# Four graph layers on one core: moving the small steps of each layer norm from GpSimd to VectorE and ScalarE

## The chip, the core and the metric

The kernel runs on one core of a Trainium2 chip. A core has TensorE for matmuls (PE in the profile; its weight loads are the row PEld), VectorE (DVE), ScalarE (ACT), GpSimd (POOL) and SyncE (SP), which here issues most of the DMA transfers. The metric is the time of one execution on the device, in microseconds (us). The kernel before the change takes 5522.48 us, the median of three runs (5521.77 to 5525.03). Everything is float32.

## The reference

A batch of 128 graphs, each with 128 nodes of 512 features, goes through four layers. Each layer adds its result to its input and then normalises every row. Cut to what matters here:

```python
def _layernorm(x, axis=-1, eps=1e-5):
    m = jnp.mean(x, axis=axis, keepdims=True)
    v = jnp.var(x, axis=axis, keepdims=True)
    return (x - m) / jnp.sqrt(v + eps)

def hypergraph_conv(x, adj, W, b):            # used twice in layer 1
    H = (adj != 0).astype(x.dtype)
    w = adj.reshape(N, -1)[:, :C]             # the first row of adj
    xw = jnp.einsum('ncd,hd->nch', x, W)
    Dn = jnp.einsum('nce,ne->nc', H, w);  Dn = jnp.where(Dn > 0, 1.0 / Dn, 0.0)
    Be = H.sum(axis=1);                   Be = jnp.where(Be > 0, 1.0 / Be, 0.0)
    m = Be[:, :, None] * jnp.einsum('nce,nch->neh', H, xw)
    return Dn[:, :, None] * jnp.einsum('nce,neh->nch', H, m) + b

# layer 1
h = jax.nn.relu(hypergraph_conv(x, adj, W1, b1))      # 1024 wide
h = layer_norm(h, gamma, beta)                        # a norm inside the layer
y = hypergraph_conv(h, adj, W2, b2)
x = _layernorm(x + (y + x))
# layers 0, 2 and 3 (two attention-like graph layers and one of 8 heads): x = _layernorm(x + layer(x, adj))
```

Each graph therefore has five norms (one for each layer and one inside layer 1), 640 in all, each over 128 rows, one row in a partition.

## The kernel before

The program works on pairs of graphs (`U = 2`), 64 pairs, and two pairs at a time. Matrix products are done by Strassen's scheme, which trades matmuls for additions: GpSimd builds sums of the left operands (`operands`, `lefts`), and VectorE or ScalarE takes each product out of PSUM into its block of the result.

The instructions are not issued in the order of the source. A `Plan` records every operation with its engine, an estimate of its length and its dependencies; a list scheduler then plays all engines forward and puts each engine's instructions in a fixed order. Every operation is emitted from one line (L369), so the profile is read by the names of tiles, not by lines. A name such as `four`, `first`, `out`, `ks` or `rows` is a piece of memory that holds different things at different times; `col` holds numbers, one or a few to each row; `bank` and `t` are PSUM.

The norm, and the part of it that GpSimd has:

```python
def norm_terms(st, n=1):
    mv = col(2)
    ve.bn_aggr(mv, st[:, :6 * n])                                   # mean, variance
    rstd = col(1)
    po.tensor_scalar(rstd, mv[:, 1:2], EPS, None, op0=OP.add)
    po.tensor_tensor(rstd, rstd, neghalf, OP.pow)                   # (var + eps) ** -0.5
    nmr = col(1)
    po.tensor_scalar(nmr, mv[:, 0:1], rstd, -1.0, op0=OP.mult, op1=OP.mult)
    return nmr, rstd

def layer_norm(t):
    st = col(12)
    stats(st, 0, t)                                                 # ve.bn_stats
    nmr, rstd = norm_terms(st)
    ac.activation(t, t, AF.Identity, bias=nmr, scale=rstd)          # rstd * t - mean * rstd
```

Layer 1 (`...` marks cuts). `drds` holds, for each row, the factor of `bw2`, which is the row that `beta` gives behind `W2`:

```python
def prepare1():
    ...
    sp.dma_start(b2h, rows(b2, D))
    ve.tensor_scalar(b2h, b2h, 0.5, None, op0=OP.mult)
    ...
def layer1(i0):
    ...
        for b in range(U):          # HT = (adj != 0), cnt = its sums
            ve.tensor_scalar(HT[:, b], AT[:, b], 0.0, None, op0=OP.not_equal, op1=OP.add,
                                    accum_out=cnt[:, b:b + 1])
        po.tensor_scalar(cnt, cnt, 1.0, None, op0=OP.max)
        po.tensor_tensor(cnt, cnt, minus1, OP.pow)
        HB = sq(M)
        for b in range(U):
            po.tensor_scalar(HB[:, b, :P], HT[:, b], cnt[:, b:b + 1], None, op0=OP.mult)
    ...
        for b in range(U):          # the inner part of the layer, on h of 1024
            t = h[r][b].rearrange("p g f -> p (g f)")
            ve.scalar_tensor_tensor(t, t, dns[r][b], rows1[:, :2]..., op0=OP.mult, op1=OP.add)
            ac.activation(t, t, AF.Relu)
            ...                     # bn_stats of two halves
            nmr, rstd = norm_terms(sts, 2)
            ac.activation(t, t, AF.Identity, bias=nmr, scale=rstd)
    ...
        q = four()
        for b in range(U):
            po.tensor_tensor(x1[:, b], x1[:, b], b2h, OP.add)
            ac.mul(q[:, b], bw2, drds[r][:, b:b + 1])
            ve.scalar_tensor_tensor(q[:, b], x1[:, b], 2.0, q[:, b], op0=OP.mult, op1=OP.add)
        for b in range(U):
            p = bank()
            pe.matmul(p, K[:, b, :P], G[:, b], start=True, stop=True)
            ve.scalar_tensor_tensor(q[:, b], p, dns[r][b], q[:, b], op0=OP.mult, op1=OP.add)
            layer_norm(q[:, b])
```

Of the kernel before, what the change touches and what calls it, by code (L numbers as in the profile page):

```python
# [14 lines left out]
OP = mybir.AluOpType  # L15
# [3 lines left out]
D = 512  # L19
# [6 lines left out]
EPS = 1e-5  # L26
U = 2
# [9 lines left out]
WHENT = (.8, 2.1), (2.0, 3.1)  # L37
WHEN1 = (-3.0, -2.3, -1.6, -1.1, .2, .6)
STEP1 = .22
WHENH, WHENW, WHENG = (2.4, 3.0), (2.8, 3.5), (3.4, 4.1)  # L40
WHEN2 = (-2.4, -2.0, -1.45, -1.15, -.7, .3, .5, 2)
WHENV, WHENS, WHENP, WHENO = (.9, 1.9), (2.2, 3.2), (3, 4), (3.5, 4.5)
LAG1, LAG2 = 1, 1.5
# [74 lines left out]
def estimate(engine, name, out, args, kw):  # L118

    n = out.idx.size if isinstance(out, View) else 0  # L120
    views = [a for a in args if isinstance(a, View)]
    psum = any(a.tile.kind in PSUM for a in views)
    scalars = sum(isinstance(a, View) and a.idx.size == 1 for k, a in [*enumerate(args), *kw.items()] if k != "accum_out")
    if engine == PE:
        return 107 if name == "transpose" else (1.74 if n <= P else 1.68) * n
    if name == "dma_start":
        return ISSUE
    if engine == DVE:
        if name == "bn_aggr":
            return 75  # L130
        if name == "reciprocal":
            return 67 + 6.5 * n
        if name in ("tensor_reduce", "bn_stats"):
            n = views[0].idx.size
        fast = name in ("tensor_scalar", "tensor_copy") and not psum and "accum_out" not in kw
        return 67 + n / (1.92 if fast else .96) + (61 * scalars if n > 8 else 0)
    if engine == ACT:
        return 50 + n / 1.2 + (0 if psum else 43) + 92 * scalars + 94 * ("accum_out" in kw)
    if name == "tensor_tensor":
        return 500 + 35 * n if OP.pow in args else 150 + 2.1 * n if n < 800 else 1.82 * n  # L140
    return 40 if name == "memset" else 180 + 3.2 * n if n > 8 else 180


def shares_port(engine, name, args, kw):
# [227 lines left out]
def rows(ap, n):  # L372

    return bass.AP(tensor=ap.tensor, offset=ap.offset, ap=[[0, P], [1, n]])
# [3 lines left out]
def kernel(  # L378
# [41 lines left out]
    for kind, k, t in (*(("out", k, t) for k, t in enumerate(outs)), ("w28", 0, places["w28"][0]),  # L420
                       ("row1", 0, places["row1"][0])):
        for c in range(SIZE[kind] // SIZE["four"]):
# [3 lines left out]
    pe, ve, ac, po, sp = (plan.engine(*e) for e in ((PE, nc.tensor), (DVE, nc.vector), (ACT, nc.scalar),  # L426
                                                     (POOL, nc.gpsimd), (SP, nc.sync)))

    def tile_of(kind, *shape):
        n = math.prod(shape)  # L430
        flat = View(Tile(kind), np.arange(SIZE[kind]))[:, :n]
        names = [f"a{k}" for k in range(len(shape))]
        return flat if len(shape) == 1 else flat.rearrange(
            f"p ({' '.join(names)}) -> p {' '.join(names)}", **dict(zip(names, shape)))

    def fixed(*shape, name, kind="fixed"):
        t = const.tile([P, *shape], FP, name=name)
        return View(Tile(kind, t), np.arange(math.prod(shape)).reshape(shape))
# [4 lines left out]
    def four():  # L443

        return tile_of("four", U, D)
# [4 lines left out]
    def col(*n):  # L450
        return tile_of("col", *n)
# [3 lines left out]
    ident = View(Tile("fixed", ident_), np.arange(P))  # L455
    neghalf = fixed(1, name="neghalf")
    po.memset(neghalf, -0.5)
    minus1 = fixed(U, name="minus1")
    po.memset(minus1, -1.0)
    tiny = fixed(1, name="tiny")  # L460
    po.memset(tiny, 1e-12)
    junk = fixed(D, name="junk", kind="free")
# [1 line left out]
    def dot(dst, u, v, n=D):  # L464
        ve.scalar_tensor_tensor(junk[:, :n], u, 1.0, v, op0=OP.mult, op1=OP.mult, accum_out=dst)
# [25 lines left out]
    def seven(nk, nh):  # L491

        return tile_of("w28", 7, nk, nh)

    def combine(W, on=ve):

        on.tensor_tensor(W[:, T3], W[:, B22], W[:, B12], OP.subtract)
        on.tensor_tensor(W[:, T1], W[:, B12], W[:, B11], OP.subtract)
        on.tensor_tensor(W[:, T2], W[:, B22], W[:, T1], OP.subtract)
        on.tensor_tensor(W[:, N4], W[:, B21], W[:, T2], OP.subtract)  # L500
# [140 lines left out]
    def norm_terms(st, n=1):  # L641
        mv = col(2)
        ve.bn_aggr(mv, st[:, :6 * n])
        rstd = col(1)
        po.tensor_scalar(rstd, mv[:, 1:2], EPS, None, op0=OP.add)
        po.tensor_tensor(rstd, rstd, neghalf, OP.pow)
        nmr = col(1)
        po.tensor_scalar(nmr, mv[:, 0:1], rstd, -1.0, op0=OP.mult, op1=OP.mult)
        return nmr, rstd

    def layer_norm(t):
# [315 lines left out]

    rows1 = tile_of("row1", 4, D)
    b1_b = [rows1[:, k] for k in range(2)]
    b2h = rows1[:, 2]  # L970
    bw2 = rows1[:, 3]

    def prepare1():
        for g in range(2):
            sp.dma_start(b1_b[g], rows(b1[g * D:(g + 1) * D], D))
        sp.dma_start(b2h, rows(b2, D))
        ve.tensor_scalar(b2h, b2h, 0.5, None, op0=OP.mult)
        WT["w1"] = Seven([four() for _ in range(7)])
        yield from load_T(WT["w1"], [w1], 2, D)
        for k, j in enumerate((B11, B21, T2, T1, B22, T3, N4)):  # L980
            yield
            WT["w1"].tiles[j] = Split(WT["w1"].tiles[j], tile_of("q3", 3, 2 * P))
            combine(WT["w1"].tiles[j], (ve, po)[k % 2])
        WT["w1"] = WT["w1"].tiles
        gb = four().rearrange("p u f -> p (u f)")
        sp.dma_start(gb, rows(gamma, DH))
        bb = four().rearrange("p u f -> p (u f)")
        sp.dma_start(bb, rows(beta, DH))
        cols = fixed(C, name="cols1")
        two = fixed(C, 2, name="two")  # L990

        def gamma_beta(o, st):
            for g in range(2):
                dot(two[:, o, g:g + 1], st[:, g * D:(g + 1) * D], bb[:, g * D:(g + 1) * D])
            ve.tensor_tensor(st, st, gb, OP.mult)

        WT["w2"] = seven(4, D // 2)
        yield from load_T(WT["w2"], [w2], 4, D // 2, gamma_beta, True)
        ve.tensor_reduce(cols, two, AX.X, OP.add)
        spread(bw2, cols)  # L1000

    def each(*lists):

        base = plan.key
        for r, args in enumerate(zip(*lists)):
            plan.key = base + r
            yield args

    def layer1(i0):
# [5 lines left out]
        for (_, ab), in each(loaded):  # L1015
            AT = sq()
            turned(AT, ab)
            HT = sq()
            cnt = col(U)
            for b in range(U):  # L1020
                ve.tensor_scalar(HT[:, b], AT[:, b], 0.0, None, op0=OP.not_equal, op1=OP.add,
                                        accum_out=cnt[:, b:b + 1])
            po.tensor_scalar(cnt, cnt, 1.0, None, op0=OP.max)
            po.tensor_tensor(cnt, cnt, minus1, OP.pow)
            HB = sq(M)
            for b in range(U):
                po.tensor_scalar(HB[:, b, :P], HT[:, b], cnt[:, b:b + 1], None, op0=OP.mult)
            po.tensor_copy(HB[:, :, P:P + 1], AT[:, :, 0:1])
            po.memset(HB[:, :, P + 1:P + 2], 1.0)
            HTs.append(HT)  # L1030
            HBs.append(HB)
        yield
        Ks, kept, dns, drds = [], [], [], []
# [42 lines left out]
        for r, i in enumerate(both):  # L1076
            plan.key = base + STEP1 * (5, 7)[r]
            for b in range(U):
                t = h[r][b].rearrange("p g f -> p (g f)")
                ve.scalar_tensor_tensor(t, t, dns[r][b], rows1[:, :2].rearrange("p g f -> p (g f)"),  # L1080
                                        op0=OP.mult, op1=OP.add)
# [4 lines left out]
                nmr, rstd = norm_terms(sts, 2)  # L1086
                ac.activation(t, t, AF.Identity, bias=nmr, scale=rstd)
                loads.append(through_dram(h[r][b].rearrange("p (j g) (k w) -> p j (g k) w", j=1, k=2), f"h{i + b}"))
        for r, i in enumerate(both):
            plan.key = base + WHENH[r]  # L1090
            hT = []
            for b in range(U):
                t = four().rearrange("p g (c n) -> p g c n", n=P)
                turned(t.rearrange("p g c n -> p (g c) n"), loads[U * r + b]())
                hT.append(t)
            ops = operands(hT[0][:, 0], hT[0][:, 1], hT[1][:, 0], hT[1][:, 1])
            plan.key = base + WHENW[r]
            G = four()
            strassen(ops, WT["w2"], 4, D // 2, plain_take(*halves(G)))
            plan.key = base + WHENG[r]  # L1100
            x1 = load_rows(x1d[i // U])
            K = tile_of("k", U, M)
            sp.dma_start(K.rearrange("p b n -> p (b n)"), kept[r], run=U * M)

            q = four()
            for b in range(U):
                po.tensor_tensor(x1[:, b], x1[:, b], b2h, OP.add)
                ac.mul(q[:, b], bw2, drds[r][:, b:b + 1])
                ve.scalar_tensor_tensor(q[:, b], x1[:, b], 2.0, q[:, b], op0=OP.mult, op1=OP.add)
            for b in range(U):  # L1110
                p = bank()
# [3 lines that stand above are left out]
            sp.dma_start(x2d[i // U], q)  # L1115
# [213 lines left out]
    n = B // U  # L1329
# [57 lines left out]
```

## Time and profile before

The profiled execution has a span of 5528.7 us at a mean TensorE clock of 0.992.

| engine | busy, us | share of the span | instructions |
|---|---|---|---|
| PE, matmuls | 5368.3 | 97% | 29145 |
| PEld, weight loads | 4254.2 | 77% | 29145 |
| DVE | 4386.7 | 79% | 10018 |
| ACT | 2317.8 | 42% | 5967 |
| POOL | 4585.9 | 83% | 6372 |

The layers follow each other with some overlap. Layer 0 ends and layer 1 begins around 1330 us, layer 1 gives way to layers 2 and 3 around 3080 us, and those two run together to the end. Two things help in reading. A busy time counts a stretch once, also where two instructions overlap; the mean length of a group counts each instruction whole. And a float32 matmul stands in the trace as two records, so that a count of matmuls there is twice that of the program.

### The profile page before, as it was taken

What the parts mean: (1) busy time and instruction counts of PE and PEld (TensorE: products, weight loads), DVE (VectorE), ACT (ScalarE), POOL (GpSimd) and SP (SyncE); (2) the same over time, 40 slices, a digit from 0 to 9 for tenths busy, and PEclk for the clock granted to TensorE, in tenths of its full rate; (3) what the DMA queues carried; (4) which work ended last, traced back from release to release, by engine and by line L of the source; (5) the groups of instructions that cost most, each with busy time, mean ns of one, the idle gap of its engine ahead of it and who ended that gap; (6) DMA issues with size and microseconds to landing.
All of it is one profiled execution on the core that took longest, in us unless ns stands there. A gap on an engine that the chain in (4) does not pass through costs nothing.

```text
span 5528.7 us, 93993 instructions
## 1 busy us (share of the span) xinstructions
PE 5368.3 (97%) x29145; PEld 4254.2 (77%) x29145; DVE 4386.7 (79%) x10018; ACT 2317.8 (42%) x5967; POOL 4585.9 (83%) x6372
## 2 busy tenths in 40 slices
PE   8999999999899999999999899999999999999998
PEld 4555555555688888888888788888898889898897
DVE  6787888877888888888788877777777777877776
ACT  2333333333344444444444334444444444444444
POOL 6777777767899999999999778888888888888886
PEclk8999999999999999999999999999999999999999
DMA  3333333334454545454545545555555555555553
GB/s 91 105 96 97 100 97 104 98 106 120 127 161 132 167 134 162 130 167 134 162 132 160 167 132 161 153 160 154 156 165 153 155 163 151 159 164 153 155 152 124
DMA packets 788378, 768.33 MB, mean 139 GB/s; under 512 B 264859, under 2 KB 592547, under 8 KB 787878
## 3 DMA queue, kind: packets, MB, share of 16 engines
q1 hardware_dynamic: 786374, 759.71, 45.8%
q8 instruction: 232, 3.80, 0.3%
q10 hardware_dynamic: 1504, 2.62, 0.2%
q14 instruction: 268, 2.20, 0.1%
HBM read 435.83 MB, written 326.24 MB: 138 GB/s over the span
## 4 chain that ended last, share of the span: by engine, by line
PE 76%; POOL 7%; DVE 6%; DMA 5%; issue 3%; ACT 2%; SPq 1%; POOLq 0%; DVEq 0%; ACTq 0%
PE bank L369 58%; PE t L369 18%; POOL out L369 2%; POOL four L369 2%; DVE first L369 2%; DVE out L369 2%; POOL col L369 1%; DVE col L369 1%; POOL first L369 1%; DMA out<-h 1%; SPq L369 1%; DVE four L369 1%; DMA four<-in_x_dram 1%; DMA four<-h 1%; DVE sq L369 1%
## 5 line engine op out<-in xcount | busy, mean ns | idle before, releaser
L369 PE MATMUL bank<-first,four 128*128 128x386 f32 (+3 forms) x4804 | 1464.8, 449 | 40.9 <-DVE out L369 23.1
L369 PEld LDWEIGHTS bank<-first,four 128*128 128x128 f32 (+2 forms) x4804 | 852.8, 189 | 601.1 <-DVE out L369 138.0
L369 DVE TENSOR_TENSOR out<-bank,out 128x386 f32<-128x386 f32 (+1 forms) x1968 | 960.3, 505 | 333.8 <-PE bank L369 250.0
L369 DVE TENSOR_TENSOR first<-bank,first 128x256 f32<-128x256 f32 x1351 | 546.3, 415 | 141.7 <-PE bank L369 122.9
L369 POOL TENSOR_TENSOR out<-out 128x256 f32<-128x256 f32 (+3 forms) x355 | 417.3, 1186 | 234.5 <-DVE out L369 187.2
L369 PE MATMUL bank<-first,out 128*128 128x256 f32 (+3 forms) x2414 | 560.7, 372 | 15.0 <-DVE first L369 8.5
L369 PEld LDWEIGHTS bank<-first,out 128*128 128x128 f32 (+2 forms) x2414 | 418.4, 187 | 105.6 <-DVE first L369 16.7
L369 ACT COPY out<-bank 128x258 f32<-128x258 f32 (+2 forms) x520 | 213.8, 417 | 646.6 <-PE bank L369 550.1
L369 POOL TENSOR_TENSOR col<-col,neghalf 128x1 f32<-128x1 f32 x640 | 384.1, 605 | 10.6
L369 POOL TENSOR_TENSOR four<-four,four 128x256 f32<-128x256 f32 (+2 forms) x445 | 377.6, 851 | 7.7 <-PE bank L369 0.7
L369 PE MATMUL bank<-four,out 128*128 128x256 f32 (+2 forms) x1568 | 381.0, 367 | 1.2 <-DVE first L369 0.8
L369 DVE TENSOR_TENSOR four<-bank,four 128x256 f32<-128x256 f32 x645 | 263.7, 415 | 141.1 <-PE bank L369 132.0
L369 PE MATMUL bank<-out,first 128*128 128x128 f32 (+3 forms) x2148 | 357.0, 309 | 13.1 <-ACT ks L369 2.6
L369 POOL TENSOR_TENSOR first<-first 128x512 f32<-128x512 f32 (+3 forms) x264 | 302.4, 1161 | 77.1 <-DVE first L369 56.1
L369 PE MATMUL bank<-four,first 128*128 128x128 f32 (+3 forms) x2144 | 362.9, 310 | 2.7 <-DVE rows L369 0.9
L369 ACT ACTIVATE four<-four,col,col 128x512 f32<-128x512 f32 x262 | 211.0, 812 | 312.4 <-POOL col L369 279.0
L369 POOL TENSOR_SCALAR col<-col 128x1 f32<-128x1 f32 (+1 forms) x704 | 185.4, 268 | 180.6 <-DVE col L369 136.1
L369 PEld LDWEIGHTS bank<-out,first 128*128 128x128 f32 (+2 forms) x2148 | 289.2, 186 | 45.5 <-issue 6.7
L369 PEld LDWEIGHTS bank<-four,first 128*128 128x128 f32 (+2 forms) x2144 | 301.1, 189 | 27.8 <-DVE ks L369 1.5
L369 PE MATMUL bank<-four,four 128*128 128x256 f32 (+2 forms) x1156 | 291.8, 371 | 13.2 <-DVE first L369 11.9
L369 POOL TENSOR_TENSOR four<-four 128x256 f32<-128x256 f32 (+2 forms) x375 | 275.1, 746 | 35.3 <-DVE four L369 27.9
L369 PEld LDWEIGHTS bank<-four,out 128*128 128x128 f32 (+2 forms) x1568 | 263.9, 188 | 40.4 <-issue 3.2
(448 smaller groups left out, 13190.6 us busy)
## 6 DMA issues: line engine op xcount, KB each, us to landing
h<-first SPq DMA_DIRECT2D x496, 128.0 KB, 2.6
out<-x1d SPq DMA_DIRECT2D x94, 512.0 KB, 5.0
out<-h SPq DMA_DIRECT2D x79, 512.0 KB, 4.8
four<-in_x_dram SPq DMA_DIRECT2D x512, 64.0 KB, 2.0
four<-in_x_dram SPq DMA_DIRECT2D x63, 512.0 KB, 4.0
x1d<-four SPq DMA_DIRECT2D x63, 512.0 KB, 2.8
first<-S SPq DMA_DIRECT2D x55, 512.0 KB, 4.2
four<-h SPq DMA_DIRECT2D x49, 512.0 KB, 4.7
```

The costliest lines, as they stand in the source:

```text
L369: call(*map(real, args), **{n: real(a) for n, a in kw.items()})
```

## The change

Of the small steps of each norm only the power stays on GpSimd. The addition of eps and the change of the mean's sign go to VectorE, in place, and the product of the mean and the inverse deviation goes to ScalarE. In layer 1, the inverse of the counts is made by VectorE with a maximum and a reciprocal. The row that is added to each node there (`b2` and the multiple of `bw2`) is built by one VectorE instruction, which takes the place of an addition on GpSimd and a product on ScalarE. The aim is to free GpSimd of many short instructions. The estimates that the scheduler uses and two of its starting times in layer 1 are changed with it, so that the order of the instructions is dealt anew on every engine.

```diff
-WHENH, WHENW, WHENG = (2.4, 3.0), (2.8, 3.5), (3.4, 4.1)
+WHENH, WHENW, WHENG = (2.4, 3.0), (2.9, 3.6), (3.6, 4.3)
...
         if name == "bn_aggr":
-            return 75
+            return 95
...
-    return 40 if name == "memset" else 180 + 3.2 * n if n > 8 else 180
+    return 60 if name == "memset" else 180 + 3.2 * n if n > 8 else 215
...
     def norm_terms(st, n=1):
         mv = col(2)
         ve.bn_aggr(mv, st[:, :6 * n])
+        ve.tensor_scalar(mv[:, 1:2], mv[:, 1:2], EPS, None, op0=OP.add)
+        ve.tensor_scalar(mv[:, 0:1], mv[:, 0:1], -1.0, None, op0=OP.mult)
         rstd = col(1)
-        po.tensor_scalar(rstd, mv[:, 1:2], EPS, None, op0=OP.add)
-        po.tensor_tensor(rstd, rstd, neghalf, OP.pow)
+        po.tensor_tensor(rstd, mv[:, 1:2], neghalf, OP.pow)
         nmr = col(1)
-        po.tensor_scalar(nmr, mv[:, 0:1], rstd, -1.0, op0=OP.mult, op1=OP.mult)
+        ac.mul(nmr, mv[:, 0:1], rstd)
         return nmr, rstd
...
-            po.tensor_scalar(cnt, cnt, 1.0, None, op0=OP.max)
-            po.tensor_tensor(cnt, cnt, minus1, OP.pow)
+            ve.tensor_scalar(cnt, cnt, 1.0, None, op0=OP.max)
+            ve.reciprocal(cnt, cnt)
...
             for b in range(U):
-                po.tensor_tensor(x1[:, b], x1[:, b], b2h, OP.add)
-                ac.mul(q[:, b], bw2, drds[r][:, b:b + 1])
+                ve.scalar_tensor_tensor(q[:, b], bw2, drds[r][:, b:b + 1], b2_b, op0=OP.mult, op1=OP.add)
                 ve.scalar_tensor_tensor(q[:, b], x1[:, b], 2.0, q[:, b], op0=OP.mult, op1=OP.add)
```

(`b2_b` is the row `b2` as it is loaded; the halving of it in `prepare1`, and the constant `minus1`, go away.)

More of the change, by code (lines that the diff above doesn't have):

```diff
@@ L457 @@
     po.memset(neghalf, -0.5)
-    minus1 = fixed(U, name="minus1")
-    po.memset(minus1, -1.0)
     tiny = fixed(1, name="tiny")
@@ L969 @@
     b1_b = [rows1[:, k] for k in range(2)]
-    b2h = rows1[:, 2]
+    b2_b = rows1[:, 2]
     bw2 = rows1[:, 3]
@@ L975, in prepare1 @@
             sp.dma_start(b1_b[g], rows(b1[g * D:(g + 1) * D], D))
-        sp.dma_start(b2h, rows(b2, D))
-        ve.tensor_scalar(b2h, b2h, 0.5, None, op0=OP.mult)
+        sp.dma_start(b2_b, rows(b2, D))
         WT["w1"] = Seven([four() for _ in range(7)])
```

## The prediction

> **What bounds the kernel now.** I read the engine totals first. PE is busy for 97% of the span, so the change can win only from what PE loses, and not from the time it takes off GpSimd. Then I ask where PE loses. The forty slices of the page (138 us each) give the stages:
>
> ```profile
> PE   8999999999899999999999899999999999999998
> DVE  6787888877888888888788877777777777877776
> POOL 6777777767899999999999778888888888888886
> ```
>
> POOL stands at 9 from the twelfth to the twenty-second slice, which is layer 1, and lower elsewhere. Next I took the busy time in stretches from the middle of each layer (stretch, length, then the engines):
>
> ```profile
> 130.00:1200.00 1070.00, 1063.67 (x3154) 571.64 (x3153) 858.23 (x2003) 412.64 (x907) 766.54 (x1070) 1.00 0.34 99
> ...
> 1420.00:2900.00 1480.00, 1449.56 (x6926) 1216.96 (x6924) 1211.67 (x2643) 609.31 (x1018) 1403.57 (x1974) 1.00 0.49 148
> ...
> 3200.00:5400.00 2200.00, 2169.67 (x15926) 1957.41 (x15925) 1721.68 (x4091) 1001.80 (x3385) 1833.80 (x2542) 1.00 0.51 155
> ```
>
> PE idles 6, 30 and 30 us in them; 94 of its 160 idle us lie in the starts, the hand-overs and the end. POOL is at 72%, **95%** and 83%, DVE at 80%, 82% and 78%. Busy PE is not PE at full pace: the timeline shows 8 weight loads, each with a 256-column record, in 1.70 us, 0.83 ns for a column. By that pace the columns of the records in the layer 1 stretch need 1408 us, so 72 us (4.9%) are lost, against 1036 of 1070 us (3.2%) in layer 0. (In layers 2 and 3 small matmuls run side by side, and this count fails.) The waits of the weight loads in the layer 1 stretch tell for whom:
>
> ```profile
> PEld bank L369 <- issue: 31.5, 112, 1.9
> PEld bank L369 <- DVE first L369: 21.5, 39, 2.1
> PEld bank L369 <- DVE out L369: 12.5, 12, 2.5
> ...
> PEld bank L369 <- POOL out L369: 8.1, 14, 1.0
> PEld bank L369 <- POOL col L369: 6.3, 12, 2.0
> ```
>
> All POOL rows of that answer sum to 21 us, all DVE rows to 47. So PE waits there more for VectorE than for GpSimd.
>
> **What the Trainium skill says.** "Perfetto Trace Analysis", Identifying the Most-Contended Engine, warns that matmul busy time is a poor measure and points to weight loads; the trace agrees, with 30 us idle but 72 us lost. "SBUF — State Buffer", Who interferes with whom: a VectorE instruction with two SBUF tensors contends with a GpSimd instruction that reads SBUF. The 128x1024 scalar_tensor_tensor on `rows` fits: 1229 ns at least, 1603 on average, 3085 at most. "ScalarE: Activation LUTs", What ACT_TABLE_LOAD costs: 186 ns for immediate operands and about 93 for each pointer operand, an estimate of 280 ns for the new product; the trace has 294 ns for a 128x2 ACTIVATE with a pointer bias. "GPSIMD Engine Reference", 3.1: about 156 ns of dispatch in every instruction; the shortest 128x1 step here took 203 ns.
>
> **The change part by part.** The rows for it, from the groups with shapes kept apart (count, then busy us and mean ns):
>
> ```profile
> L369 POOL TENSOR_TENSOR col<-col,neghalf 128x1 f32<-128x1 f32 x640 | 384.1, 605 | 10.6
> L369 POOL TENSOR_SCALAR col<-col,col 128x1 f32<-128x1 f32 x640 | 184.2, 292 | 43.1
> L369 POOL TENSOR_SCALAR col<-col 128x1 f32<-128x1 f32 x640 | 168.6, 268 | 162.3 <-DVE col L369 133.5
> L369 POOL TENSOR_TENSOR out<-out,rows 128x512 f32<-128x512 f32 x92 | 121.1, 1319 | 0.0
> L369 POOL TENSOR_TENSOR col<-col,minus 128x2 f32<-128x2 f32 x64 | 53.1, 830 | 0.0
> ...
> L369 DVE SCALAR_TENSOR_TENSOR out<-out,out 128x512 f32<-128x512 f32 x50 | 44.2, 885 | 0.1
> L369 DVE RECIPROCAL col<-col 128x2 f32<-128x2 f32 x192 | 30.3, 158 | 4.2 <-ACT col L369 1.6
> ```
>
> 1. Off GpSimd: the two TENSOR_SCALARs of each norm, 168.6 + 184.2 = 353 us; of the counts, the power 53.1 and a maximum 16.8, 70 us; the `b2h` additions, 64 pairs x 2 x 1.32 us = 169 us. Sum 592 us of lengths. As neighbours on POOL overlap by some 40 ns, about 515 us of busy time: 4586 to **4070 us, 74%**. In the layer 1 stretch (212 norms, 53 pairs): 212 x 2 x 0.235 + 53 x 1.0 + 106 x 1.29 = 290 us, 1404 to 1114, **75%** instead of 95%.
>
> 2. Onto VectorE: 1280 steps of one column. A short instruction lasts some 155 ns by its row, but the next starts 80 ns before its end (the timeline has an aggregate of 0.17 us at 2001.44 and its successor at 2001.52), so it holds the engine for 75: 96 us. In the new order the eps step stands right behind its aggregate in some 130 cases and waits out those 80 ns: 10 us. Maximum and reciprocal: 64 x 0.155 = 10 us. The new row: 128 x (885 - 75 ns) = 104 us. Together 220; less contention with a freer GpSimd gives back perhaps 20. DVE goes from 4387 to about **4590 us, 83%**; in the layer 1 stretch by 212 x 2 x 0.075 + 8 + 106 x 0.81 - 15 = 111 us, to 1320 us, **89%**.
>
> 3. ScalarE: 640 products, each about 0.2 us of the engine next to the activation that follows; less 128 products of 717 ns (64.3 + 21.3 us in the rows `out<-rows` and `four<-rows`). Net +50, up to 2370 us, 43%: no bound.
>
> 4. The chain of a norm. At the end of the span the aggregate begins at 5516.15, and POOL's three steps at 5516.41, 5516.72 and 5517.38, the activation at 5517.68: 1.53 us. After: aggregate 0.17, sign and eps 0.15, a hop of 0.1, power 0.57, a hop, product 0.25: some 1.4 us. The chain itself hardly shrinks; what shrinks is the queueing, as it enters POOL's in-order queue once instead of three steps deep, behind additions of 0.7 to 1.8 us. ACT waits 623 us for `POOL col` in all, but ACT is 58% idle, so little of that is on PE's path.
>
> The sum for PE. Its work is the same, 14789 instructions in both orders. In layer 1 I take away half of the 21 us that PE waits for POOL and some 10 us of the waits for VectorE that begin with a late operand or a contended port, in the stretch; the rest of the layer (about 10% more) and its crowded start give 4. Against it stand 89% of VectorE, which must also empty the banks: +8 us. Layer 0 and layers 2 and 3: POOL was no bound there, about 0. Net about -16 us: 5522.5 - 16 = **5507 us**, a gain of 0.3%.
>
> **The rivals.**
> (a) *VectorE becomes the bound of layer 1.* For it: PE already waits there twice as long for DVE as for POOL, and DVE goes to 89%, near what POOL had. Against it: the added instructions wait for nothing that is late, the row can be built early, and the starting times of the late stages were moved back. It would make 5530 to 5550.
> (b) *GpSimd was hidden anyway.* For it: the scheduler puts the operands well ahead, and even at 95% POOL is named for only 21 us. Then 5518 to 5525.
> (c) *GpSimd was the pace of layer 1, and its queue the reason also for the DVE and issue waits.* Then the loss falls from 4.9% to layer 0's 3.2% or less: 1.7% of 1640 us is 28 us, and with a quicker hand-over up to 45: 5478 to 5495.
> (d) *The new order* moves waits about by itself, also in stages that the change hardly touches, by perhaps 10 us either way.
>
> **Range and chances.** Half of my weight lies between (b) and (c), a quarter on each side. The ends come from (c) with luck in (d), 5475, and a mild (a), 5540. Two per cent is 110 us; faster by that much would need more than two thirds of all that PE idles, and slower by that much more than the whole of the added VectorE load of layer 1 on PE's path. Both get 0.01.
>
> **What would show it.** POOL near 4070 and DVE near 4590 us on the page; in the layer 1 stretch POOL near 75%, DVE near 89%, PE's loss of 72 us down to about 55; fewer waits of weight loads for POOL there. Wrong if the DVE rows of those waits grow by more than the POOL rows fall (rival a), if layer 1 is unchanged (b), or if the time moves in layer 0 or in layers 2 and 3, which would be the order alone (d). In step 2 the weak number is 885 ns for the new row, in step 4 the share of waits that I gave to POOL.

## The result, and the profile after

The changed kernel takes 5480.41 us (median of 4 runs, 5479.22 to 5485.4) against 5523.75 us before (with a fourth run of it): a ratio of **0.9923, with a 95% interval of 0.9905 to 0.994**. That is 43 us less, where 16 were predicted; the time lies within the range, near its low end.

The slices of the changed kernel (137 us each, the same three rows as before):

```profile
PE   7999999999999999999999999999999999999998
...
DVE  6888887878998899998999978777778777877876
...
POOL 6666666666777777777777567777777777777776
```

The row of nines has left POOL, and layer 1 (from the eleventh slice to the twenty-third) has them on DVE instead, with three eights among them: the two engines have changed places. By the page POOL is busy for 4037.1 us (74%), DVE for 4549.0 (83%), ACT for 2397.3 (44%). In the layer 1 stretch:

```profile
1420.00:2900.00 1480.00, 1454.12 (x6949) 1223.14 (x6948) 1340.76 (x3319) 601.09 (x1130) 1157.03 (x1351) 1.00 0.50 150
```

POOL falls from 95% to 78% of it, DVE rises from 82% to 91%. Yet PE gains only 5 us of busy time in this stretch. The waits of its weight loads there say why (for whom, us in total, times, longest):

```profile
PEld bank L369 <- DVE first L369: 38.2, 76, 1.4
PEld bank L369 <- issue: 21.7, 88, 0.7
PEld t L369 <- DVE first L369: 15.5, 31, 1.2
PEld bank L369 <- DVE col L369: 12.3, 10, 2.2
```

All POOL rows of that answer now sum to 5 us instead of 21, all DVE rows to 71 instead of 47, issue to 29 instead of 42. With the few of ACT and DMA, the sum is 112 us; it was 115. Inside layer 1 the waits for GpSimd have become waits for VectorE.

To see where the 51 us between the two profiled spans come from, I add up the columns of PE's records at 5/6 ns (0.83) each. All of them make 5316 us in every kernel here, as the matmuls are the same; so the time at which a given share of that work is done can be compared. Work 0 to 1200 us is layer 0 with the start; 1200 to 3100 is layer 1 with both hand-overs; the rest is layers 2 and 3.

| kernel (profiled span, us) | layer 0 | layer 1 and hand-overs | layers 2 and 3 |
|---|---|---|---|
| before (5528.7) | 1293.1 | 2058.5 | 2177.0 |
| after (5477.4) | 1290.7 | 2037.0 | 2149.7 |
| difference | -2.4 | -21.5 | -27.3 |

Of the 21.5 us of layer 1, 11 come at its beginning (work 1200 to 1350), 9 at its end (2700 to 3100), and only 2 between. And more than half of the whole gain lies in **layers 2 and 3**, where I had put nothing. Every stage length here is from one profiled execution. That of before took 5530.45 us, where its other executions in this document lie between 5514.58 and 5533.12; so differences of a few us between stages say nothing.

### The profile page after: what moved, and what is told of

Same layout as the page of the kernel before. It is cut to its first block, busy times and chain, and to the rows that moved or that the text cites. A ratio compares the mean times of both kernels' runs of the same rounds, so it can differ in the third digit from the quotient of the medians.

```text
span 5477.4 us, 94041 instructions
## 1 busy us (share of the span) xinstructions
PE 5346.1 (98%) x29145; PEld 4258.7 (78%) x29145; DVE 4549.0 (83%) x11553; ACT 2397.3 (44%) x6479; POOL 4037.1 (74%) x4835
## 4 chain that ended last, share of the span: by engine, by line
PE 56%; DVE 7%; DMA 3%; POOL 2%; issue 1%; ACT 1%; SPq 1%; DVEq 0%; POOLq 0%; ACTq 0%
PE bank L369 42%; PE t L369 14%; DVE first L369 2%; DVE col L369 2%; DVE out L369 1%; DVE four L369 1%; POOL out L369 1%; SPq L369 1%; DMA out<-h 1%; DMA h<-first 1%; DMA out<-x3d 1%; POOL first L369 0%; DMA first<-x3d 0%; ACT first L369 0%; DVE junk L369 0%
## 5 line engine op out<-in xcount | busy, mean ns | idle before, releaser
L369 PE MATMUL bank<-first,out 128*128 128x256 f32 (+2 forms) x2560 | 623.4, 381 | 25.7 <-DVE first L369 10.1
L369 PEld LDWEIGHTS bank<-first,out 128*128 128x128 f32 (+1 forms) x2560 | 469.4, 190 | 127.3 <-DVE first L369 30.6
L369 PE MATMUL bank<-four,out 128*128 128x256 f32 (+2 forms) x2118 | 538.1, 376 | 2.9 <-DVE col L369 1.4
L369 PE MATMUL bank<-out,first 128*128 128x128 f32 (+2 forms) x2840 | 427.8, 290 | 2.2 <-DVE out L369 1.2
L369 PEld LDWEIGHTS bank<-out,first 128*128 128x128 f32 (+1 forms) x2840 | 374.4, 188 | 26.0 <-DVE four L369 2.8
L369 ACT ACTIVATE col<-col,col 128x1 f32<-128x1 f32 x640 | 183.2, 292 | 456.2 <-POOL col L369 390.1
L369 ACT COPY t<-out 128x512 f32<-128x512 f32 x256 | 150.2, 591 | 421.9 <-DVE four L369 217.6
L369 POOL TENSOR_TENSOR out<-out,out 128x256 f32<-128x256 f32 (+2 forms) x286 | 288.2, 1011 | 9.3 <-DVE four L369 4.4
L369 POOL TENSOR_SCALAR sq<-sq,col 128x128 f32<-128x128 f32 x256 | 160.5, 636 | 153.4 <-DVE col L369 149.0
L369 DVE BATCH_NORM_STATS2 col<-first 128x6 f32<-128x512 f32 x370 | 245.5, 681 | 27.2 <-ACT first L369 25.4
```

The source lines that it names most:

```text
L369: call(*map(real, args), **{n: real(a) for n, a in kw.items()})
```

## Experiments

Twelve kernels ran, in three groups of four, each group beside the kernel before, whose medians there were 5526.18, 5523.83 and 5525.55 us. Every ratio is to those.

**1. The same order, the norm's steps moved.** The scheduler still plans the operations of before, but what is emitted at their places is that of the change:

```diff
+        op = plan.ops[-1]                      # the aggregate: eps and sign are emitted with it
+        op[1] += [(nc.vector.tensor_scalar, (mv[:, 1:2], mv[:, 1:2], EPS, None), dict(op0=OP.add)),
+                  (nc.vector.tensor_scalar, (mv[:, 0:1], mv[:, 0:1], -1.0, None), dict(op0=OP.mult))]
         po.tensor_scalar(rstd, mv[:, 1:2], EPS, None, op0=OP.add)
+        plan.ops[-1][1] = []                   # planned, not emitted; so too the last product
...                                             # the activation's place emits the product first
```

> The order of the kernel before on every engine, with the three small steps of each norm placed as in the change: eps and sign on VectorE right behind the aggregate, the power alone on GpSimd, the product on ScalarE right ahead of its activation. Counts and the added row stay as before. Theory A (the load taken off GpSimd makes the gain, whatever the order): 5485 to 5505 us, with layers 2 and 3 some 20 us shorter. Theory B (the new order makes it): 5515 to 5530 us, no stage shorter by over 5 us.

Measured: 5573.42 us, ratio 1.0089 (1.0072 to 1.0106). Neither theory: it is *slower* by 47 us, 14 of them in layer 0 and 27 in layer 1. Layers 2 and 3, where GpSimd lost the same small steps, gain nothing (2181 us against 2177). In layer 0 the weight loads wait 19 us more for VectorE (118.0 against 98.8 in the stretch 130 to 1200). Its 128 norms cost 14 us, 0.11 us each. By the starts in this trace (medians of layer 0) the eps step follows its aggregate after 205 ns, where the next step of before followed after 89, and eps and sign then hold VectorE for 71 and 61: about 0.25 us for each norm. So something under half of it lands on PE, if all of the loss is VectorE's, which is not shown: the power and the product have moved too.

**2. The order of the change, the norm's steps back on GpSimd.** The converse: the plan is that of the changed kernel; at the place of the power GpSimd does all three steps, and the places on VectorE and ScalarE stay empty.

> The order of the changed kernel on every engine, with the small steps of each norm put back on GpSimd, at the place of the power. Theory A (load): the gain of layers 2 and 3 is lost again, 5505 to 5525 us, PE waits for POOL's numbers again. Theory B (order): stays at 5480 to 5490 us.

Measured: 5562.4 us, 1.0071 (1.0056 to 1.0086), 82 us above the changed kernel. Load and order can't be had apart: an order that is dealt for one placement loses with the other, in both directions. Both theories, as I had put them, fall: the time lies above either range.

**3. The norm alone**, dealt anew (the norm's part of the diff on the kernel before, nothing else).

> The kernel before with the change of the norm alone; counts, added row, estimates and starting times as before, the order dealt anew. Theory A (load): 5485 to 5500 us, nearly the whole gain of layers 2 and 3 (some 27 us) and of layer 0 (some 4 us). Theory B (order is luck): anywhere within 5490 to 5530 us, with the stages moving without regard to where the load fell. Theory C (it is the layer 1 part that gains): 5515 to 5525 us.

Measured: 5520.26 us, 0.999 (0.9981 to 0.9998). The part that gives the change its name gains at most 0.2%. GpSimd is relieved by nearly 400 us in all, layers 2 and 3 are 22 us shorter, and layer 1 is 5 us longer (the profiled execution, 5514.36 us, was the shortest of twelve). The busy times in the layer 1 stretch:

```profile
1420.00:2900.00 1480.00, 1440.72 (x6857) 1208.60 (x6857) 1229.60 (x3054) 666.40 (x1219) 1257.93 (x1543) 1.00 0.49 147
```

**4. Layer 1's part alone**, dealt anew (counts and added row from the diff, norms on GpSimd).

> The kernel before with the counts and the added row of layer 1 moved to VectorE; the norm, estimates and starting times as before, the order dealt anew. Theory A (load): layer 1 and its hand-overs up to 15 us shorter, layers 2 and 3 as before, 5508 to 5522 us. Theory B (order is luck): layers 2 and 3 move too, by 10 us or more, though nothing of them is changed. Theory C: nearly all of the gain, under 5495 us.

Measured: 5481.42 us, 0.9925 (0.991 to 0.994): **the whole gain**, with a third of the relief. 24 us are from layer 1. But another 24 are from layers 2 and 3, of which this kernel changes no operation. Theory C is right by the total, and theory B by that stage. The busy times in the layer 1 stretch:

```profile
1420.00:2900.00 1480.00, 1463.95 (x6960) 1219.72 (x6959) 1285.89 (x2883) 554.12 (x918) 1266.42 (x1786) 1.00 0.51 150
```

**5. The same order, layer 1's part moved**, emitted at the places of the plan of before as in the first run:

```diff
             po.tensor_tensor(x1[:, b], x1[:, b], b2h, OP.add)
+            plan.ops[-1][1] = []
             ac.mul(q[:, b], bw2, drds[r][:, b:b + 1])
+            plan.ops[-1][1] = []
             ve.scalar_tensor_tensor(q[:, b], x1[:, b], 2.0, q[:, b], op0=OP.mult, op1=OP.add)
+            plan.ops[-1][1].insert(0, ...)     # q = bw2 * drd + b2 on VectorE, just ahead
```

> The order of the kernel before on every engine, with layer 1's part alone moved: VectorE makes the inverse counts right behind the counts and builds the added row at the place of its own last step; GpSimd's maximum, power and additions and ScalarE's products fall away without replacement. The norms stay on GpSimd. Theory A (GpSimd's load in layer 1 is what PE pays for): layer 1 and its hand-overs 10 to 20 us shorter, the rest unchanged, 5500 to 5518 us. Theory B (the gain is only in the order that is dealt to fit): 5525 to 5545 us, layers 2 and 3 within 5 us of before.

Measured: 5590.34 us, 1.0119 (1.0104 to 1.0135); layer 1 is 63 us longer. The busy times in its layer 1 stretch:

```profile
1420.00:2900.00 1480.00, 1420.44 (x6714) 1180.60 (x6713) 1303.56 (x2771) 524.98 (x883) 1222.87 (x1713) 1.00 0.48 143
```

And rows of the waits of its weight loads there:

```profile
PEld bank L369 <- DVE first L369: 46.9, 63, 3.2
...
PEld t L369 <- DVE first L369: 13.0, 16, 2.3
PEld bank L369 <- DVE out L369: 12.2, 12, 2.2
PEld bank L369 <- POOL out L369: 11.7, 16, 1.8
```

GpSimd has as much relief as in run 4 (1223 us busy here, 1266 there), and yet PE waits 85 us for VectorE instead of 47, and 32 us for GpSimd instead of 21. The relief alone, in the old order, buys nothing. The likely reason is the two long VectorE steps that now stand in a row, ahead of PSUM blocks that have to be taken out; no run isolates it.

**6 and 7. Two other deals of the kernel before**, with no operation changed:

```diff
-SLACK = 60
+SLACK = 50        # and 70 in the other
```

> The kernel before with no operation changed; the scheduler alone has a slack of 50 in place of 60, so that the order is dealt anew. Theory B (the order of before is an unlucky one in layers 2 and 3): layers 2 and 3 some 20 us shorter, 5490 to 5515 us in all. If the gain needs GpSimd's relief: 5518 to 5535 us.

> As with the slack of 50, but with 70: a second deal of the order with the operations of before. Theory B: within 5485 to 5535 us, and the two deals differ from each other by 10 us or more. If the gain needs GpSimd's relief: 5518 to 5535 us, no gain in layers 2 and 3.

Measured: 5523.46 us, 0.9999 (0.999 to 1.0008), and 5569.97 us, 1.0084 (1.0069 to 1.0099). The first lies in the range for GpSimd's relief, the second above every range that I gave. The same operations make 5523 or 5570 us, by their order alone. With 50, layers 2 and 3 are 14 us shorter and layer 0 is 11 us longer.

**8. Another deal of the changed kernel**, with a slack of 50.

> The changed kernel with no operation changed, a slack of 50 in place of 60. If the change itself makes the gain: 5475 to 5490 us. Theory B (a lucky deal): 5490 to 5525 us, with layers 2 and 3 longer by 10 us or more than in the changed kernel.

Measured: 5470.29 us, 0.9903 (0.9888 to 0.9917). A little below the range: the gain is no lucky deal of the changed kernel; this one is better.

**9. GpSimd's additions of half of `b2` left out**, so that `b2` is missing from the result; nothing is put in their place on any engine.

```diff
-                po.tensor_tensor(x1[:, b], x1[:, b], b2h, OP.add)
```

> The kernel before without GpSimd's 128 additions of half of b2 in layer 1 (they are left out, not replaced, so b2 is missing from the result); ScalarE's products and VectorE's steps stay, VectorE gets nothing. The order is dealt anew. If the freed GpSimd in layer 1 is what makes the gain of that layer: layer 1 with its hand-overs at least 20 us shorter, 5480 to 5505 us. If the gain comes from the row's other shape (no hand-over from GpSimd and ScalarE): layer 1 within 10 us of before, 5505 to 5535 us.

Measured: 5459.5 us, 0.9876 (0.986 to 0.9893); layer 1 is 41 us shorter. The busy times in its layer 1 stretch:

```profile
1420.00:2900.00 1480.00, 1464.69 (x7017) 1230.66 (x7016) 1186.33 (x2685) 628.91 (x1030) 1283.70 (x1906) 1.00 0.50 151
```

And the first four rows of the waits of its weight loads there:

```profile
PEld bank L369 <- issue: 35.5, 144, 1.4
PEld bank L369 <- DVE first L369: 28.6, 64, 2.1
PEld t L369 <- DVE first L369: 15.9, 34, 1.2
PEld t L369 <- issue: 10.8, 45, 0.2
```

PE is busy for 15 us more than before, the waits for POOL are gone (0.2 us left, the only row), and the DVE rows stay about where they were (51 us). The time is below both ranges. GpSimd's 128 additions were what layer 1 paid for: taken away, with nothing added anywhere, they give the largest gain of all. How they cost PE is not separated. GpSimd's time is one way; another is that VectorE's next step had to wait for each of them; a third is that they slowed VectorE, whose busy time over the span fell from 4386.7 to 4318.1 us with the same operations (4406 to 4429 in three other deals of the kernel before).

**10. The added row alone**, dealt anew; the counts stay on GpSimd.

> The kernel before with the added row of layer 1 alone moved to VectorE; the counts stay on GpSimd, norms, estimates and starting times as before, the order dealt anew. If the row makes the gain: layer 1 some 20 us shorter, 5475 to 5500 us. If the counts do: 5510 to 5530 us.

Measured: 5484.55 us, 0.9925 (0.991 to 0.994); layer 1 is 26 us shorter. The counts are not needed for the gain.

**11. All operations of the change, with the old estimates and starting times.**

> All operations of the changed kernel, with the scheduler's estimates and starting times of the kernel before. If the operations make the gain: 5470 to 5490 us. If the starting times and estimates carry a part of it: 5490 to 5520 us, with layer 1 longer than in the changed kernel.

Measured: 5465.05 us, 0.9888 (0.9874 to 0.9903). Below the range: it beats both kernels, and layer 1 takes 2017 us instead of the changed kernel's 2037.

**12. The new estimates and starting times alone.**

> The operations of the kernel before with the new estimates and starting times: one more deal of its order. If estimates and starting times gain nothing by themselves: within the spread of the other deals of these operations, 5515 to 5575 us. If they carry the gain: under 5500 us.

Measured: 5551.18 us, 1.0046 (1.0031 to 1.0061). Waits for POOL in its layer 1 stretch:

```profile
PEld bank L369 <- POOL out L369: 19.2, 16, 4.1
...
PEld bank L369 <- POOL four L369: 13.0, 11, 2.2
```

The POOL rows sum to 51 us. The tuning that came with the change gains nothing by itself, and by run 11 it did not help the change either.

**All deals side by side** (stage lengths in us, without the three kernels that keep a foreign order):

| kernel | layer 1 and hand-overs | layers 2 and 3 |
|---|---|---|
| additions on GpSimd: before, slack 50, slack 70, constants alone | 2059, 2052, 2080, 2096 | 2177, 2163, 2180, 2154 |
| the same, norms moved (norm alone) | 2064 | 2155 |
| additions off GpSimd, norms there: layer 1's part, row alone, left out | 2035, 2032, 2017 | 2153, 2162, 2151 |
| both off: after, its slack 50, old constants | 2037, 2018, 2017 | 2150, 2157, 2150 |

In **layer 1** the five with the additions on GpSimd take 2052 to 2096 us and the six without take 2017 to 2037: the groups don't overlap. In **layers 2 and 3** the seven deals with the norms on GpSimd have the very same operations, and lie between 2151 and 2180. The kernel before is the second longest of them; against their mean of 2163 us, the changed kernel's stage is 13 us shorter and not 27.

## Why the prediction was right, and where it was not

*What bounds the kernel*: right. PE's work is the same, and the gain came from its waits.

*Steps 1 to 3, the loads*: right. POOL 4037 us (4070 foretold), DVE 4549 (4590), ACT 2397 (2370); in the stretch POOL 78% (75%) and DVE 91% (89%). Two sums in them were loose. For POOL, the 1536 steps that go, at the 40 ns of overlap that I named, make 61 us, so 531 us of busy time and not 515; it fell by 549. For ACT my own terms give 42 us, not 50; it rose by 79, as a product costs it some 0.24 us (run 3 adds 155 us for 640) where I took 0.2. The rows after, from the groups of the changed kernel:

```profile
L369 DVE TENSOR_SCALAR col<-col 128x1 f32<-128x1 f32 x1280 | 136.5, 142 | 4.7
...
L369 DVE SCALAR_TENSOR_TENSOR out<-rows,col 128x512 f32<-128x512 f32 x82 | 66.2, 824 | 0.0
...
L369 DVE SCALAR_TENSOR_TENSOR four<-rows,col 128x512 f32<-128x512 f32 x44 | 45.0, 1034 | 0.0
```

A small step lasts 142 ns, and by the starts in the trace the next follows after 61 (median) instead of my 75. The new row takes 895 ns on average over all 128, against the 885 that I called the weak number. My 20 us for the freer GpSimd can't be read from one deal: the 128x1024 step on `rows` went from 1601 to 1661 ns on average, the 128x128 step on `sq` from 390 to 346; and with the operations of before the first averages anything from 1362 (run 12) to 1849 (run 7), by the order alone.

*Step 4, the chain*: right. At the end of the span:

```profile
5468.16 0.17 DVE L369 BATCH_NORM_AGGREGATE col<-col 128x2 f32<-128x6 f32 x1
...
5468.36 0.21 DVE L369 TENSOR_SCALAR col<-col 128x1 f32<-128x1 f32 x2
...
5468.60 0.55 POOL L369 TENSOR_TENSOR col<-col,neghalf 128x1 f32<-128x1 f32 x1 [2.90 <-DVE col L369]
...
5469.18 0.29 ACT L369 ACTIVATE col<-col,col 128x1 f32<-128x1 f32 x1 [2.31 <-POOL col L369]
...
5469.51 0.81 ACT L369 ACTIVATE first<-first,col,col 128x512 f32<-128x512 f32 x1
```

From the aggregate to the activation 1.35 us, against 1.53 before and 1.4 foretold. As I said there, little of it is on PE's path: the norm alone gains next to nothing.

*The sum for PE*: right in sign, wrong in its terms. Three were mis-sized.

- In the stretch I took half of the 21 us of POOL waits and 10 us of DVE waits away. POOL waits fell by 16, but DVE waits rose by 24; the loss of 72 us became about 67, not 55. By my own sign of being wrong, rival (a) is real inside layer 1, and only the fall of the other waits held it level.
- To the rest of layer 1 I gave 4 us; the hand-overs gave 20. Run 9 shows that such a gain follows from GpSimd's additions alone (25 of its 41 us lie there). Why it comes at the hand-overs in the changed kernel was not settled.
- To layers 2 and 3 I gave "about 0", and to rival (d) "perhaps 10 us either way". This is the step that failed, and that stage's gain was a sign of being wrong that I had named. A new deal of the same operations moves that stage within 29 us and the whole kernel by 46 (run 7). The 27 us of layers 2 and 3 are little more than what layer 1's part brought there (24) without touching them. So it was partly luck that the time fell inside the range: more than half of the gain came from where my sum had none, and the range was wide enough for it through (c) and (d).

*The rivals*: (b) falls, as run 9 shows. (c) had the right total with part of the right cause: by runs 10 and 9 the additions on GpSimd in layer 1 did cost PE some 25 to 40 us, but the norms' small steps there, as far as run 3 shows, nothing. (d) is right in kind, and at its largest over four times what I gave it.

**Open**: why the norms' relief of GpSimd (1258 us busy in the stretch of run 3) gave layer 1 nothing, where that of the additions (1284 in run 9) gave 41 us. It is one deal, and deals differ by 44 us in this stage. Open also is whether the moved norms help layers 2 and 3: four deals with them average 2153 us, seven without 2163, and the seven alone spread over 29.

## What to carry to other kernels

Where a scheduler deals the instructions anew after every edit, an edit's gain is not read from one build: deal it a few times without changing an operation, and only then ask which part of the gain is more than that spread. Ask of each part of a change alone, and with the order dealt to fit it: here the small part that was named last (the added row) made the gain of layer 1 and the part in the title, alone, made next to none. And an engine with room on average may still have none just ahead of the instructions that empty PSUM.

## What the runs showed that I had not expected

An order that was dealt for another placement of the same work cost 0.7% to 1.2% against the kernel before, three times out of three (5562, 5573 and 5590 us). In the last of them GpSimd was relieved from 95% to 83% of the stretch and VectorE rose to only 88%, and still PE waited 85 us for VectorE instead of 47: with the order of every engine fixed, the place of a load in it counted here for more than its sum.
